# Steps of the norms' transpositions, the MLP's first weights, and the loads of attention's first position terms, placed anew in a four-layer vision kernel

## The chip, the cores and the metric

One core of a Trainium2 chip runs the whole program. The metric is the device time of one execution in microseconds (us), as the median of several runs. A core has five engines that run side by side, each with its own queue of instructions: TensorE (PE in the profile; PEld is its loading of weights), VectorE (DVE), ScalarE (ACT), GpSimd (POOL) and SyncE (SP), which here issues nearly all DMAs. Work moves between HBM and the on-chip SBUF by DMA. Products are accumulated in PSUM[...].

## The reference

The input is one image of 48 x 48 tokens (T = 2304) with C = 768 channels. Four layers follow each other, all in f32. The change touches the first, and three loads of the third.

```python
# layer 0: a transformer block, 12 heads of 64
xn  = layernorm(x, ln1_g, ln1_b)
q, k, v = split(xn @ qkv_w + qkv_b)
attn = (q * scale) @ k.T + rel_h[..., :, None] + rel_w[..., None, :]
out = softmax(attn) @ v
x   = x + out @ proj_w + proj_b
xn2 = layernorm(x, ln2_g, ln2_b)
x   = x + gelu(xn2 @ mlp_w1 + mlp_b1) @ mlp_w2 + mlp_b2     # 768 -> 3072 -> 768
# layer 1: rfft2, a block-diagonal complex MLP over 8 blocks of 96, softshrink, irfft2, + x
# layer 2: projections of x, then 12 steps of a 3x3 depthwise convolution with gates, and an output product
# layer 3: as layer 1
```

`rel_h` and `rel_w` are products of q with windows of two small tables of relative positions.

## The kernel before

**Blocks and products.** Tokens go in six blocks of TB = 384; two of them make a superblock, sb = 0, 1, 2. Each large product is taken as a 2 x 2 block product with seven multiplications instead of eight, so operands need sums of blocks first (`block_sums`, `combine`: four additions each), and results are put together on DVE from PSUM. `rows_in_seven` (L167) is this for the v product and for the output projection: seven products n = 0 to 6, three row tiles t each, so 21 calls a superblock. A call is three 128x384 products, which the profile counts as six PE instructions, into one of six PSUM tiles, an eviction by DVE or ACT, and then `between()`. After n = 1, 4, 5 and 6 `emit` adds on POOL and stores.

**Norms.** A layer norm of one block is made of `layernorm_rows` for three row tiles of 128 tokens (two statistics L74, small operations L76 to L89, one subtraction and multiplication L90, nearly all on DVE) and of `transpose_norm` (L94): for each of six channel groups, three transpositions on PE (`n_tp`) into one PSUM tile, and an eviction by ACT or DVE in turn that applies gain and bias. `prepare` does both for one block.

**qkv (`qkv_phase`, L258).** For each superblock the v product is followed by `q_and_k`: six pairs of heads `pr`, seven products n each. In sb = 0 the pair's weights are loaded and combined on POOL in place (L359 to L366), and are kept in HBM for the later superblocks. The position terms' products (`rel_h` L488, `rel_w` L480) are steps in a list that `advance()` takes one by one, after products n = 2 and 5 of pairs from pr = 2 on, and between the calls of the v product. `rel_h` fills the tile `rh` (one buffer, L491) and stores it. `prepare(sb + 1, 0)` stands after pair 3 and `prepare(sb + 1, 1)` after pair 5 (L411 to L417). x comes in six tiles of one buffer each, from a pool inside this phase (L290).

**Into attention.** `load_ahead` (L1457) loads the first keys and values at pair 4 of the last superblock. Past the last pair it opens a pool `at_a` for two query tiles `qt` and three tiles of position terms `bt` and loads them (L1464 to L1469). A bound on the scores, from the maxima of q and k, gives `flag` (L557 to L561), after which the last steps of position terms are issued (L562). Every engine reads `flag` and branches (L1487, L1488) to `attention_bounded` or `attention_any`; the given data take the first. Attention works on products of keys and queries (L657), position terms by a one-hot matrix (L667), exponentials on ACT (L669), and products with values (L688).

**Projection and MLP.** `proj_phase` (L835) makes 63 calls of `rows_in_seven` and stores x with the residual in `xr_d`. `mlp_phase` (L920) opens its pools, and calls `prepare(0, 0)`, `prepare(0, 1)`, which load rows of `xr_d`. `first_layer` (L970) loads the weights of step f (L980) and multiplies (L996).

**What sets the order.** The program gives instructions in source order. The framework's scheduler then orders each engine's queue by source order and by when it expects operands and buffers to be free, so that an instruction can come out ahead of its line's place; `tc.keep_in_program_order` pins one. Tiles of one tag share the given number of buffers, and memory of a closed pool is given to pools opened later. It is the scheduler too that puts in the waits.

## Time and profile before

| | us |
|---|---|
| median of 3 runs (lowest, highest) | 3575.01 (3571.93, 3576.77) |
| the profiled execution | 3578.66 |
| its span, first to last instruction | 3576.8 |

| stage, us from the span's start | length | PE busy |
|---|---|---|
| qkv phase and entry, 0 to 461 | 461 | 446.4 |
| attention, 461 to 1470 | 1009 | 1006.8 |
| projection, 1470 to 1597 | 127 | 122.8 |
| entry to the MLP, 1597 to 1622 | 25 | 18.1 |
| MLP, 1622 to 2595 | 973 | 973.0 |
| layer 1, 2595 to 2845 | 250 | 245.6 |
| layers 2 and 3, 2845 to 3577 | 732 | 701.0 |

In the timeline's lines below, the first two columns are start and length in us; then come the engine, the line of the kernel, the operation, the tiles written and read, the shape, and the count. In brackets stands the time that the engine sat idle before, and what ended it. PE busy counts instructions in flight: at a low granted clock an instruction takes longer, and PE still counts as busy. Times of the profile are of one execution.

### The profile page before, as it was taken

To read this page: it belongs to the slowest core of one execution; us is meant where nothing else is said; L and a number is where in the kernel's file an instruction comes from. 1 tells how busy PE (TensorE), PEld (TensorE's weight loads), DVE (VectorE), ACT (ScalarE), POOL (GpSimd) and SP (SyncE) were. 2 spreads that over 40 slices of the span, in tenths; PEclk is the share of its full clock that TensorE was granted. 3 is DMA by queue.
4 is the path that set the end of the run, shared out by engine and by line. 5 is a ranking of instruction groups with operands and counts; after the bars stand their busy time and mean duration, and the time that the engine had idled before them with its cause. 6 is when DMAs were issued, how large, how long until landed. Compare 5 with 4: busy or idle time off the path is not lost.

```text
span 3576.8 us, 52953 instructions
## 1 busy us (share of the span) xinstructions
PE 3513.7 (98%) x21274; PEld 2148.0 (60%) x21274; DVE 2004.7 (56%) x3015; ACT 1141.4 (32%) x1735; POOL 680.8 (19%) x572
## 2 busy tenths in 40 slices
PE   9999999999999999989999999999999998999998
PEld 5666554444444444555555555555578767996685
DVE  7644466766676776654234324232345578996554
ACT  1321254555555555203101210121023265223332
POOL 3211102111111110250000000000023303981121
PEclk9999999999999999999999999999999999999999
DMA  7555556655545443344346334533554403104456
GB/s 276 201 187 189 187 156 173 187 145 152 164 123 148 125 125 87 111 150 139 106 131 184 114 110 126 164 112 112 156 134 119 109 21 105 34 27 100 107 143 132
DMA packets 281171, 480.38 MB, mean 134 GB/s; under 512 B 37250, under 2 KB 234466, under 8 KB 274708
## 3 DMA queue, kind: packets, MB, share of 16 engines
q1 hardware_dynamic: 265322, 455.95, 43.8%
q10 hardware_dynamic: 15594, 20.94, 2.0%
q8 instruction: 171, 2.80, 0.3%
q14 instruction: 84, 0.69, 0.1%
HBM read 330.82 MB, written 145.98 MB: 133 GB/s over the span
## 4 chain that ended last, share of the span: by engine, by line
PE 91%; DVE 3%; POOL 2%; DMA 2%; ACT 1%; issue 1%; SPq 0%; ACTq 0%; DVEq 0%; POOLq 0%
PE p L996 14%; PE p L1059 13%; PE s L657 12%; PE av L688 12%; PE qk L375 6%; PE c L1223 4%; PE s L667 3%; PE c L1323 3%; PE v L180 3%; PE pj L180 3%; PE f_u L1682 2%; PE f_z L1666 2%; PE f_z L1667 2%; PE so L1410 2%; PE f_x L1631 2%; POOL t L1331 1%
## 5 line engine op out<-in xcount | busy, mean ns | idle before, releaser
L677 DVE TENSOR_TENSOR acc<-acc,p 128x928 f32<-128x928 f32 (+1 forms) x480 | 560.2, 1167 | 263.6 <-ACT p L669 222.6
L669 ACT ACTIVATE p<-s 128x928 f32<-128x928 f32 (+1 forms) x540 | 506.5, 940 | 491.6 <-PE s L667 470.0
L657 PE MATMUL s<-qt,kv 64*128 64x464 f32 (+1 forms) x2160 | 521.9, 559 | 7.5 <-DMA qt<-q_d 5.5
L1059 PE MATMUL p<-w,h 128*128 128x384 f32 x1512 | 492.3, 486 | 0.0
L688 PE MATMUL av<-p,kv 128*64 128x464 f32 (+1 forms) x2160 | 442.9, 554 | 0.0
L1059 PEld LDWEIGHTS p<-w,h 128*128 128x128 f32 x1512 | 285.6, 190 | 199.0 <-issue 4.2
L667 PE MATMUL s<-bt,oneh 64*128 64x464 f32 (+1 forms) x1080 | 400.8, 731 | 0.7 <-DMA bt<-rh_d 0.7
L688 PEld LDWEIGHTS av<-p,kv 128*64 128x64 f32 x2160 | 147.0, 137 | 261.9 <-issue 249.6
L657 PEld LDWEIGHTS s<-qt,kv 64*128 64x128 f32 x2160 | 203.0, 187 | 164.7 <-issue 153.4
L996 PE MATMUL p<-x2nT,w 128*128 128x384 f32 x864 | 294.0, 491 | 4.0 <-POOL rr L1035 4.0
L1323 PE MATMUL c<-H,bands 128*48 128x96 f32 x5632 | 245.1, 247 | 10.2 <-DVE th L1261 8.3
L375 PE MATMUL qk<-xnT,wqk 128*128 128x384 f32 x756 | 249.8, 487 | 0.3 <-DMA wqk<-wqk_d 0.3
L1323 PEld LDWEIGHTS c<-H,bands 128*48 128x48 f32 x5632 | 235.2, 124 | 20.3 <-issue 8.7
L996 PEld LDWEIGHTS p<-x2nT,w 128*128 128x128 f32 x864 | 165.2, 192 | 121.3 <-POOL rr L1035 4.2
L996 PE MATMUL p<-xT,w 128*128 128x384 f32 x648 | 220.8, 486 | 0.0
L1035 POOL TENSOR_TENSOR rr<-rr,ml_b 128x1152 f32<-128x1152 f32 x12 | 31.8, 2653 | 946.1 <-DMA rr<-xr_d 855.1
L991 ACT ACTIVATE h<-h,ml_b 128x384 f32<-128x384 f32 x144 | 88.5, 616 | 346.7 <-DVE h L1011 173.5
L375 PEld LDWEIGHTS qk<-xnT,wqk 128*128 128x128 f32 x756 | 141.4, 190 | 93.4 <-issue 0.9
L1331 POOL TENSOR_TENSOR t<-s,c 128x768 f32<-128x768 f32 x80 | 144.4, 1829 | 179.4 <-DVE s L1294 166.5
L996 PEld LDWEIGHTS p<-xT,w 128*128 128x128 f32 x648 | 123.1, 190 | 85.9
L667 PEld LDWEIGHTS s<-bt,oneh 64*128 64x128 f32 x1080 | 106.9, 188 | 105.7 <-issue 102.9
L1666 PE MATMUL f_z<-f_w,f_o 97*96 97x96 f32 x800 | 134.1, 249 | 0.0
(336 smaller groups left out, 4601.2 us busy)
## 6 DMA issues: line engine op xcount, KB each, us to landing
w<-w1s_d SPq DMA_DIRECT2D x36, 768.0 KB
w<-w2s_d SPq DMA_DIRECT2D x36, 768.0 KB
w<-w1s_d SPq DMA_DIRECT2D x36, 576.0 KB
w<-in_mlp_w_dram SPq DMA_DIRECT2D x27, 768.0 KB
yu<-f_ys SPq DMA_DIRECT2D x48, 384.0 KB
wqk<-wqk_d SPq DMA_DIRECT2D x12, 1344.0 KB
bt<-rw_d SPq DMA_DIRECT2D x72, 174.0 KB
bt<-rh_d SPq DMA_DIRECT2D x72, 174.0 KB
```

Source lines behind the costliest of these rows:

```text
L180: nc.tensor.matmul(p[:, :TB], lhsT=rhs[n][:, c, t * P : (t + 1) * P], rhs=w[:, c, :], start=c == 0, stop=c == NC2 - 1)
L375: nc.tensor.matmul(p[:, :TB], lhsT=w[:, n, c, :], rhs=ops[sb][n][:, c, :], start=c == 0, stop=c == NC2 - 1)
L657: nc.tensor.matmul(ps[:, s, :n], lhsT=keys[pr % 2][rows, kt * P : (kt + 1) * P], rhs=held(c)[rows, :n], start=True, stop=False)
L667: nc.tensor.matmul(ps[:, s, :n], lhsT=oneh[rows, b % 2, :], rhs=bts[b // 2][rows, j, :n], start=False, stop=True)
L669: nc.scalar.activation(p, ps[:, :, :n], AF.Exp)
L677: nc.vector.tensor_tensor(probs[c], probs[c], p, ALU.add)
L688: nc.tensor.matmul(avs[c][rows, : size(c)], lhsT=vals[pr % 2][:, kt, rows], rhs=p[:, s, :], start=kt == 0, stop=kt == NT - 1)
L996: nc.tensor.matmul(p[:, :TB], lhsT=w[n][:, c, :], rhs=rhs[n][:, c, :], start=c == 0, stop=c == NC2 - 1)
L1059: nc.tensor.matmul(ps[t][:, :TB], lhsT=hs[left, f][:, t * P : (t + 1) * P], rhs=wt[:, f % KW2, :], start=f == 0, stop=f == NF2 - 1)
L1323: nc.tensor.matmul(ps[r0 : r0 + G, k // 4, cols], lhsT=bands[:, n - GC, i, :] if gr else bands0[:, n, i, :], rhs=H[:, n, :, d : d + NPR], ...
L1331: GP.tensor_tensor(t, sc[:, ch], c1[:, m0 : m0 + GC].unsqueeze(2).to_broadcast([P, GC, RR, NPR]), ALU.mult)
L1666: nc.tensor.matmul(out, lhsT=o1[:, j, 1:3, :].rearrange("c r h -> c (r h)"), rhs=w2t[:, b, 0, :], start=True, stop=False)
```

## The change

It does seven things.

1. `transpose_norm` becomes a generator that stops after each channel group. In the qkv phase from sb = 1 on its transpositions are pinned on PE. `q_and_k` makes the norm at pairs 1 and 3, and takes its steps after products: of pairs 2 and 4 (n = 1, 3, 4, 6), and of 3 and 5 (n = 0, 1).
2. The norm of the first MLP superblock moves into the projection, with the statistics (L74) and the transpositions pinned: `mlp_norms` holds what `mlp_phase` had, and `proj_phase` takes a step of it at the calls named in `norm_at`. The first two weights of the MLP are loaded at calls 40 and 41.
3. The tiles of x become pairs in a pool `at_x` of three buffers, which lives through attention; `bt` takes the same buffers. `qt` lies in the pool of attention's constants.
4. In the last superblock `rh` has three buffers, in the place of `rw`.
5. The last steps of position terms come ahead of the bound.
6. In sb = 0, block sums that n = 4 and later need are issued at n = 2 of the v product, the windows of the position tables are loaded after it, and the weights of pairs 0 and 1 are made in its `emit`, with POOL's additions pinned for pairs 0 to 2.
7. Three loads of biases in the scan phase (layer 2) are pinned on SP.

```diff
-def layernorm_rows(nc, pool, xt, name):
+def layernorm_rows(nc, pool, xt, name, pin=lambda ins: ins):
...
-        nc.vector.bn_stats(out=st[:, i, :], in_=xt[:, i * half : (i + 1) * half])
+        pin(nc.vector.bn_stats(out=st[:, i, :], in_=xt[:, i * half : (i + 1) * half]))
...
-def transpose_norm(nc, psum, xhs, xnT, ident, g, b, name):
+def transpose_norm(nc, psum, xhs, xnT, ident, g, b, name, pin=lambda ins: ins):
...
-            nc.tensor.transpose(ps[:, t * P : (t + 1) * P], xhs[t][:, cc * P : (cc + 1) * P], ident)
+            pin(nc.tensor.transpose(ps[:, t * P : (t + 1) * P], xhs[t][:, cc * P : (cc + 1) * P], ident))
...
+        yield
...
         wv = qkv_w.rearrange("(c p) n -> p c n", p=P)
-        Xs, ops = {}, {}
+        Xs, ops, pairs = {}, {}, [None]
...
                 i = (2 * sb + half) * 3 + t
-                Xs[i] = xp.tile([P, C], F32, tag="x", name=f"x_{i}", bufs=6)
+                if i % 2 == 0:
+                    pairs[0] = xb.tile([P, 2, C], F32, tag="xb", name=f"x_{i}")
+                Xs[i] = pairs[0][:, i % 2]
                 if i == 1:
...
-            transpose_norm(nc, lambda name: pool.tile([P, 512], F32, tag=tag, name=name), xhs, ops[sb][:, :, half, :], ident, g, b, f"n1_{blk}")
+            return transpose_norm(nc, lambda name: pool.tile([P, 512], F32, tag=tag, name=name), xhs, ops[sb][:, :, half, :], ident, g, b, f"n1_{blk}", tc.keep_in_program_order if sb else lambda ins: ins)
...
                 nc.sync.dma_start(v_d[:, 3 * blk : 3 * blk + 3, cols], o)
+                if sb == 0 and len(made) < 2:
+                    make_qk(len(made))
...
+        made = []
+        def make_qk(pr):
+            w = w_tile(f"wqk_0_{pr}").rearrange("p (n c f) -> p n c f", n=7, c=NC2)
+            wb = wp.tile([P, NC2, P], F32, tag="wb", name=f"wb_{pr}", bufs=2)
+            lo, hi = slice(pr * P, (pr + 1) * P), slice(C + pr * P, C + (pr + 1) * P)
+            nc.sync.dma_start(w[:, 0:2].rearrange("p a c f -> p (a c) f"), wv[:, :, lo])
+            nc.sync.dma_start(w[:, 6], wv[:, NC2:, hi])
+            nc.sync.dma_start(wb, wv[:, :NC2, hi])
+            pin = tc.keep_in_program_order if pr < 3 else lambda ins: ins
+            combine(nc.gpsimd, (w[:, 0], w[:, 1], wb, w[:, 6]), w[:, 3], w[:, 2], w[:, 5], w[:, 4], pin)
+            made.append(w)
...
-            made = []
...
-                    w = w_tile(f"wqk_{sb}_{pr}").rearrange("p (n c f) -> p n c f", n=7, c=NC2)
-                    wb = wp.tile([P, NC2, P], F32, tag="wb", name=f"wb_{pr}", bufs=2)
-                    lo, hi = slice(pr * P, (pr + 1) * P), slice(C + pr * P, C + (pr + 1) * P)
-                    nc.sync.dma_start(w[:, 0:2].rearrange("p a c f -> p (a c) f"), wv[:, :, lo])
-                    nc.sync.dma_start(w[:, 6], wv[:, NC2:, hi])
-                    nc.sync.dma_start(wb, wv[:, :NC2, hi])
-                    combine(nc.gpsimd, (w[:, 0], w[:, 1], wb, w[:, 6]), w[:, 3], w[:, 2], w[:, 5], w[:, 4])
-                    made.append(w)
+                    if pr > 1:
+                        make_qk(pr)
+                    w = made[pr]
...
                         step()
+                    elif sb + 1 < NSB and (pr in (2, 4) and n or pr in (3, 5) and n < 2):
+                        next(norm, None)
                 for o, d, m in ((q[:, pr], q_d, qms), (kt, k_d, kms)):
...
                     ahead(0)
-                if pr == NC2 and sb + 1 < NSB:
-                    prepare(sb + 1, 0)
-                    load_x(sb + 1, 1)
+                if pr in (1, 3) and sb + 1 < NSB:
+                    norm = prepare(sb + 1, pr // 2)
             if sb == 0:
                 nc.sync.dma_start(wqk_d[NC - 1], made[NC - 1])
-            if sb + 1 < NSB:
-                prepare(sb + 1, 1)
...
-            prepare(0, 1, first_sums)
+            finish(prepare(0, 1, first_sums))
...
-            tc.keep_in_program_order(V.tensor_tensor(w[:, 4], w[:, 1], w[:, 2], ALU.subtract))
-            tc.keep_in_program_order(V.tensor_tensor(w[:, 5], w[:, 0], a21, ALU.subtract))
-            V.tensor_tensor(x12, x22, x12, ALU.subtract)
-            V.tensor_tensor(t4, x21, t2, ALU.subtract)
...
-            windows = load_windows(nc, atc, relT)
-            tc.keep_in_program_order(V.tensor_scalar(kb, qkb[:, NC : 2 * NC], HD**-0.5, None, ALU.mult))
-            rm = qp.tile([P, 2], F32, tag="rm", name="rm")
-            tc.keep_in_program_order(V.tensor_reduce(rm, windows.rearrange("p t k s -> p t (k s)"), axis=AX.X, op=ALU.max, apply_absolute_value=True))
+            V.tensor_scalar(kb, qkb[:, NC : 2 * NC], HD**-0.5, None, ALU.mult)
...
-            v_rows(0, lambda n: w[:, n])
+            def weights(n):
+                if n == 2:
+                    V.tensor_tensor(w[:, 4], w[:, 1], w[:, 2], ALU.subtract)
+                    tc.keep_in_program_order(V.tensor_tensor(w[:, 5], w[:, 0], a21, ALU.subtract))
+                    V.tensor_tensor(x12, x22, x12, ALU.subtract)
+                    V.tensor_tensor(t4, x21, t2, ALU.subtract)
+                return w[:, n]
+            v_rows(0, weights)
+            windows = load_windows(nc, atc, kp, relT)
+            rm = qp.tile([P, 2], F32, tag="rm", name="rm")
+            V.tensor_reduce(rm, windows.rearrange("p t k s -> p t (k s)"), axis=AX.X, op=ALU.max, apply_absolute_value=True)
...
-        with tc.tile_pool(name="qkv_o", bufs=1, side="right") as op:
+        with tc.tile_pool(name="qkv_o", bufs=1, side="right") as op, ExitStack() as after:
...
+            rw_stack, pools = ExitStack(), []
+            rwp = rw_stack.enter_context(tc.tile_pool(name="qkv_r", bufs=1, side="right"))
...
                     if (n, hh) == (0, 0):
-                        tiles["rh"] = op.tile([P, KP, 2, 2, TB], F32R, tag="rh", name=f"rh_{sb}_{cp}")
+                        if sb + 1 < NSB:
+                            tiles["rh"] = op.tile([P, KP, 2, 2, TB], F32R, tag="rh", name=f"rh_{sb}_{cp}")
+                        else:
+                            if cp == 0:
+                                rw_stack.close()
+                                pools.append(after.enter_context(tc.tile_pool(name="qkv_h", bufs=3, side="right")))
+                            tiles["rh"] = pools[0].tile([P, KP, 2, 2, TB], F32R, tag="rh", name=f"rh_{sb}_{cp}")
                     by_row, at = tiles.pop(("h", cp, n, hh)), tiles["rh"]
...
+            while steps or ready:
+                advance()
...
-            while steps or ready:
-                advance()
...
+        norm_at = {28, *range(39, 45), 47, *range(56, 63)}
...
-            rows_in_seven(nc, pm, f"pj_{sb}", rhs, lambda n: w[:, n - 2] if n > 1 else pw[:, n], xp, emit)
+            calls = itertools.count(21 * sb)
+            def between():
+                n = next(calls)
+                if n in norm_at:
+                    next(norm, None)
+                if n in (40, 41):
+                    first_weights(0, n - 40)
+            rows_in_seven(nc, pm, f"pj_{sb}", rhs, lambda n: w[:, n - 2] if n > 1 else pw[:, n], xp, emit, between)
+        finish(norm)
...
-def mlp_phase(tc, ident, w1s_d, b1, w2, w2s_d, b2, ln_g, ln_b, xr_d, xa_d, follow_in):
+def mlp_norms(tc, stack, ident, ln_g, ln_b, xr_d, w1s_d):
+    nc = tc.nc
+    cp = stack.enter_context(tc.tile_pool(name="ml_c", bufs=1, side="left"))
+    pt = stack.enter_context(tc.tile_pool(name="ml_t", bufs=2, space=PSUM))
+    wp = stack.enter_context(tc.tile_pool(name="ml_w", bufs=4, side="left"))
+    g = load_cols(nc, cp, ln_g, NC, "ln2_g")
+    b = load_cols(nc, cp, ln_b, NC, "ln2_b")
+    ops, ws = {}, {}
+    def first_weights(sb, f):
+        ws[sb, f] = []
+        for i, n in enumerate(S1W):
+            wt = wp.tile([P, 4, NC2, P], F32, tag="w", name=f"w1_{sb}_{f}_{i}")
+            nc.sync.dma_start(wt[:, :n], w1s_d[f, :, 3 * i : 3 * i + n])
+            ws[sb, f] += [wt[:, k] for k in range(n)]
+    def prepare(xp, sb, half):
+        blk = 2 * sb + half
+        if half == 0:
+            ops[sb] = [cp.tile([P, NC, 2, TB], F32, tag="x2nT", name=f"x2nT_{sb}")]
+            ops[sb] += [cp.tile([P, NC2, TB], F32, tag=f"x{n}", name=f"x{n}_{sb}") for n in ("T1", "T2", "T4")]
+        xhs = []
+        for t in range(3):
+            xt = xp.tile([P, C], F32, tag="x", name=f"ml_x_{blk}_{t}", bufs=6 if sb else 4)
+            r0 = (3 * blk + t) * P
+            nc.sync.dma_start(xt, xr_d[r0 : r0 + P, :])
+            xhs.append(layernorm_rows(nc, xp, xt, f"ln2_{blk}_{t}", lambda ins: ins if sb else tc.keep_in_program_order(ins)))
+        X, t1, t2, t4 = ops[sb]
+        yield
+        yield from transpose_norm(nc, lambda name: pt.tile([P, 512], F32, tag="t", name=name), xhs, X[:, :, half, :], ident, g, b, f"n2_{blk}", lambda ins: ins if sb else tc.keep_in_program_order(ins))
+        if half:
+            ops[sb] = block_sums(nc, X, t1, t2, t4)
+    return cp, wp, pt, ops, (first_weights, ws), prepare
+def mlp_phase(tc, opened, b1, w2, w2s_d, b2, xr_d, xa_d, follow_in):
...
-                w = []
-                for i, n in enumerate(S1W):
-                    wt = wp.tile([P, 4, NC2, P], F32, tag="w", name=f"w1_{sb}_{f}_{i}")
-                    nc.sync.dma_start(wt[:, :n], w1s_d[f, :, 3 * i : 3 * i + n])
-                    w += [wt[:, k] for k in range(n)]
+                if (sb, f) not in ws:
+                    first_weights(sb, f)
+                w = ws.pop((sb, f))
...
-                bias = load_bcast(nc, wp, b0_d, NA + NCR, "bias")
-                bias1 = load_bcast(nc, tp, b1_d, NA + NCR, "u")
+                bias = load_bcast(nc, wp, b0_d, NA + NCR, "bias", pin=tc.keep_in_program_order)
+                bias1 = load_bcast(nc, tp, b1_d, NA + NCR, "u", pin=tc.keep_in_program_order)
...
-                cb = load_bcast(nc, wp, cb_d, NN, "cb")
+                cb = load_bcast(nc, wp, cb_d, NN, "cb", pin=tc.keep_in_program_order)
...
+    xb = at_stack.enter_context(tc.tile_pool(name="at_x", bufs=3, side="left"))
...
+    qbs = [atc.tile([P, QB], F32, tag=f"qt{i}", name=f"qt{i}") for i in range(2)]
...
-        pool = at_stack.enter_context(tc.tile_pool(name="at_a", bufs=1, side="left"))
-        qbs = [pool.tile([P, QB], F32, tag=f"qt{i}", name=f"qt{i}") for i in range(2)]
-        bts = [pool.tile([P, KJ, QB], F32R, tag=f"bt{g}", name=f"bt{g}") for g in range(NG3)]
+        bts = [xb.tile([P, 2 * C], F32R, tag="xb", name=f"bt{g}")[:, : KJ * QB].rearrange("p (j n) -> p j n", j=KJ) for g in range(NG3)]
...
-    proj_phase(tc, x, pw, ps_d, a["proj_b"], oT, xr_d)
+    mlp_stack = ExitStack()
+    mlp = mlp_norms(tc, mlp_stack, ident, a["ln2_g"], a["ln2_b"], xr_d, w1s_d)
+    with tc.tile_pool(name="pj_n", bufs=3, side="right") as xp:
+        proj_phase(tc, x, pw, ps_d, a["proj_b"], oT, xr_d, itertools.chain(*(mlp[-1](xp, 0, half) for half in range(2))), mlp[-2][0])
...
-    mlp_phase(tc, ident, w1s_d, a["mlp_b1"], a["mlp_w2"], w2s_d, a["mlp_b2"], a["ln2_g"], a["ln2_b"], xr_d, xa_d, follow_in)
+    mlp_phase(tc, mlp, a["mlp_b1"], a["mlp_w2"], w2s_d, a["mlp_b2"], xr_d, xa_d, follow_in)
+    mlp_stack.close()
```

`finish(steps)` runs a generator to its end. The qkv phase's first block and the later MLP norms use it.

## The prediction

> **What bounds the kernel now.** I read the page's busy times first, then the PE waits, then stage windows over the four places that the diff touches, then PE's and SP's order of time inside these.
>
> ```profile
> PE 3513.7 (98%) x21274; PEld 2148.0 (60%) x21274; DVE 2004.7 (56%) x3015; ACT 1141.4 (32%) x1735; POOL 680.8 (19%) x572
> ```
>
> PE is the bound: 3576.8 - 3513.7 = 63 us is all that it idles. The diff changes no product and no size, so it can only win PE's idle time and PE time spent at a low clock, or add to them. The windows (length; then busy us and count of PE, PEld, DVE, ACT, POOL; granted clock; DMA share; GB/s) show where both are:
>
> ```profile
> 201.92:223.14 21.22, 19.40 (x79) 11.68 (x78) 9.47 (x15) 6.79 (x11) 3.61 (x3) 1.00 0.96 337
> 436.44:460.96 24.52, 16.43 (x89) 13.26 (x87) 10.33 (x18) 10.89 (x14) 1.93 (x4) 0.79 0.80 213
> ...
> 1471.00:1597.50 126.50, 122.97 (x379) 71.46 (x379) 70.73 (x136) 6.80 (x16) 63.04 (x23) 1.00 0.49 156
> 1597.50:1609.88 12.38, 5.51 (x37) 3.70 (x36) 9.07 (x9) 4.03 (x6) 7.86 (x3) 0.97 0.77 239
> 1609.88:1620.73 10.85, 10.85 (x25) 6.13 (x26) 4.82 (x6) 3.66 (x4) 0.00 (x0) 0.72 0.53 197
> ```
>
> See the clock of 0.79 and 0.72: the second and the last look busy, but the same products take longer there. PE's order of time, into attention and into the MLP:
>
> ```profile
> 439.79 0.20 PE L558 MATMUL bound<-pz,onec 128*1 128x12 f32 x2 [1.83 <-DVE pz L552]
> 439.92 1.60 PE L496 MATMUL rh<-qh,windows 128*96 128x96 f32 x16
> 447.05 1.92 PE L657 MATMUL s<-qt,kv 64*128 64x464 f32 x4 [5.53 <-DMA qt<-q_d]
> 448.38 0.93 PE L667 MATMUL s<-bt,oneh 64*128 64x464 f32 x1
> 450.04 0.72 PE L667 MATMUL s<-bt,oneh 64*128 64x464 f32 x1 [0.72 <-DMA bt<-rh_d]
> ...
> 1536.52 6.22 PE L180 MATMUL pj<-pj_wt,oT 128*128 128x384 f32 x18 [1.39 <-DVE pj_u L185]
> ...
> 1597.50 0.82 PE L99 MATMUL n_tp<-ident,ml_x 128*128 128x128 f32 x6
> 1598.75 0.89 PE L99 MATMUL n_tp<-ident,ml_x 128*128 128x128 f32 x6 [0.43 <-ACT x2nT L103]
> ...
> 1609.88 7.13 PE L996 MATMUL p<-x2nT,w 128*128 128x384 f32 x12 [4.04 <-POOL rr L1035]
> ```
>
> and SP's issues that PE waits for there:
>
> ```profile
> 443.69 0.33 SPq L609 DMA_DIRECT2D qt<-q_d  x1
> 444.07 0.42 SPq L580 DMA_DIRECT2D bt<-rw_d  x1
> ...
> 1605.37 2.06 SPq L980 DMA_DIRECT2D w<-w1s_d  x4
> ```
>
> Attention's first loads go out at 443.69, when k's last store has landed (the chain of waits has DMA k_d<-kT, 437.88 for 5.74, then these issues): their tiles lie in memory that the qkv pools free. The MLP's first weights go out at 1605.37. The 4.04 us are put down to POOL L1035, which ends at 1609.29; no product reads rr, so I take the real wait to be these weights.
>
> **What the Trainium skill says.** "TensorE: Matmul & The Clock Gate", Part 1: about 3.4 us without work halve PE's clock, and about 3.4 us of work restore it. The trace agrees in kind: after idles of 5.53 and 4.04 us the clock is 0.79 and 0.72; after gaps of 1.4 us in the projection it is 1.00. The same page ("Architectural detail") has DVE and ACT strictly first in, first out, and PE's products too: a pinned operation that waits holds all behind it. Here DVE sat 7.54 us before L74 until ml_x landed at 1527.95. "SBUF — State Buffer", "Who interferes with whom": a DVE operation with two SBUF inputs and a reading GpSimd operation block each other for their whole length. Here L154 takes 3.78 us beside POOL's rr and 1.36 alone, and L86, 128x1, took 2.55 beside L862.
>
> **The change part by part**, against the span of 3576.8 us. One instruction of a 128x384 product costs 0.3225 us (36 in 11.61 at the start of the projection); three of a transposition's 128x128 products about 0.33 us when packed between others (six in 0.65 at 115.85).
>
> (a) First v products. PE waits 0.53 (28.13, DVE L449) and 1.31 us (35.52, DVE L189). Between 25.87 and 35.38 DVE does the windows' two copies (0.93, 0.95), the row maximum (0.53) and four sums of 1.34 before it takes up v's evictions. The change moves windows and maximum behind the v products and the four sums behind n = 1. The four sums then stand at n = 2, 5.4 us of DVE with six PSUM tiles of 1.935 us as cover. Gain 1.8. The windows are first read at 91.73, and rel's two loads now wait for an output tile, near 64: cover 25 us; without it they would hold SP's queue, where sb 1's x and pair 2's weights (issued 51.68 to 61.31 now) stand. make_qk's combinations, pinned on POOL, are 4 x 1.00 us after each v emit; the first weight is wanted at 58.84 and should be done near 38. Bounds 0 to 2.5.
>
> (b) Norm 1 of sb 1 and 2. sb 1's 36 transpositions already lie between products (115.85, 147.87) and lose nothing; the pins keep that. sb 2's run as a block from 215.47 to 223.30: 7.8 us, and 36 x 0.109 = 3.9 of it is work. Gain 3.9. They become PE's pinned steps one or three products apart (1.94 us), and an eviction takes 0.67. PE stands still if the norm is late, but its statistics stood on DVE at 38 to 48 for sb 1 while the first step comes near 90. The x pairs share three buffers, the same 18 KB; x_8 now waits for x_3 too, free at 24.5. Bounds 3 to 3.9.
>
> (c) Into attention. From 436.44 to 460.96 PE does 32 rh instructions (16 in 1.52: 3.0), the bound, and nine tiles of scores (0.99 each in steady state: 8.9); 24.5 - 11.9 = 12.6 us are lost. Afterwards bt lies in x's buffers, free since sb 1, and qt in its own, so all 13 loads can land before 440; kv's first load stands after pair 4 in the source (five pairs of 14 us after 348.96: near 419) and went out at 372.09, so SP takes such loads early. The rh tiles no longer share one buffer with a store in between (ACT waits 5.60 us at 443.45). What is late next is the flag: rh ends near 440.2 (POOL's copies, 1 us a step), bound and DVE's two operations 0.5, PE's load of the flag 0.86 (440.4 in the trace), branch 0.09: PE starts near 442. The exponential's table load (1.28) and three PSUM tiles cost about 0.5: nine tiles end at 451.4 instead of 460.96, gain 9.5. Worst: the flag now comes behind all rh and a gap of 3 us or more cools the clock (3 us, as at 1609.88 below), and bt lands at 445: gain 4. I take 8. Attention's load of q into oT stands behind the rh stores on SP; its products are wanted 20 us after the entry (nine tiles of scores, 4.8 of values, six tiles more).
>
> (d) Projection and MLP entry. From 1471.00 to 1620.73 PE does 378 + 24 product instructions (129.7) and 36 transpositions (3.9): 133.6 of 149.7, 16.1 lost. It is 3.5 in three DVE waits (1536 to 1551, where DVE is busy 27.91 of 28.05 us with six rows of norm), 8.4 of idle around the transpositions and for the weights, 3.1 of slow clock (24 instructions in 10.85 instead of 7.74), and 1 spread over the projection. In the changed kernel the first of the two norms is pinned at call 28, which ends 29 x 1.935 after 1471.0: 1527.1, when ml_x lands now (1527.95; its store's way is unchanged). The other is pinned at 47. Each is three row tiles of some 2.8 us on DVE (two L74 of 0.55, L90 of 0.67, eight small ones of 0.1 to 0.2): 8.4, beside one or two evictions of 0.56 a call. Six PSUM tiles cover 11.6 us. Transpositions go to calls 39 to 44 and 56 to 61. The weights of two MLP steps (2 x (768 + 576) KB) are issued at calls 40 and 41, on SP ahead of the second norm's loads: 2.7 MB at some 200 GB/s are 13 us, and calls 41 to 47 last as long. If they take longer, DVE waits at call 47. Block sums follow call 62: t1 is ready earlier, t3 and t2 cost 1.35 + 1.35, or 3.8 + 1.35 beside POOL's last addition; PE has two products (3.9 us) until it wants t2: up to 1.5 lost. ACT's first copy may wait for the last store (near +6.7), again under six tiles. I take 3 us left: gain 13. Bounds 6 (DVE falls 4 us behind at both norms) to 15.5.
>
> (e) The scan's three pinned loads: 1.3 us of SP issue move from 2623.9 (one waited until 2643.8) to about 2822; bias is first used at 2838.26. Gain 0, bounds -2 to +1.
>
> Sum: 1.8 + 3.9 + 8 + 13 = 26.7, taken as 26.5. Span 3576.8 - 26.5 = 3550.3. The profiled execution took 3578.66, 3.65 over the median of 3575.01; the same gain below that median is 3548.5. Ends of the terms: 30.7 gives 3544.3; 1 + 3 + 4 + 10 = 18 gives 3557. About 0.2% (7.1 us) is what a measurement of this kernel can tell from no change.
>
> **The rivals.** *Given back in the projection* (0.17): the pinned norms and transpositions put DVE behind there, and (d) brings 3 instead of 13: 3558.5, from 3555 to 3569. For it: 27.91 of 28.05, and blocks of 3.3 to 3.8 us beside POOL. Against: half as many rows at a time. *Entry still late* (0.13): bt or flag come as now, or the change's own tiles don't free the loads, (c) brings 2: 3552 to 3557, with 3554.5. For it: SP's queue is in order and the loads' line stands after the rh stores. Against: kv's load at 372.09. *Slower* (0.08): at calls 28 and 47 DVE waits for ml_x in front of PSUM's evictions. Price: beyond 11.6 us, one us of PE for each. A wait of W at each costs 2 x (W + 8.4 - 11.6); it decides against the change from W = 20 us on (33.6 lost, the gain and 7.1 more), and at 25 us gives 3548.5 + 43.6 = 3592. For it: the pins forbid DVE to go round them, and 2.7 MB of weights come just before. Against: the trace has 9.9 us from POOL's addition (1518.09) to the statistics (1527.95), most of them over before call 28.
>
> **How the numbers follow.** The forecast has 0.62, its own range 3544 to 3557. The range 3543 to 3563 takes in the late entry and most of the first rival; outside are that rival's end and the slower case, with a little of the forecast. Faster: 0.62 + 0.13 + 0.13 of the first rival = 0.88; within 0.2%: its 0.04; slower 0.08.
>
> **What would show it.** Right: no block of L99 after the projection; w1's loads near 1555; PE's first scores between 441 and 444 at a clock of 1.00; first MLP product within 1 us of the last of the projection; none of the DVE waits above. Wrong: PE waits for pinned transpositions on DVE L90, waits in the projection over 3 us, a gap of more than 4 us at the branch, or new idle after 1620, where I expect a shift alone.

## The result, and the profile after

The changed kernel took 3559.27 us (median of 6 runs, 3556.20 to 3560.74) beside 3574.76 us for the kernel before (6 runs, 3571.93 to 3576.77): a ratio of 0.9953, 95% interval 0.9943 to 0.9963. It is 15.5 us faster. Forecast were 26.5 us; 3559.27 lies inside the range of 3543 to 3563, but outside the likeliest case's own 3544 to 3557.

The profiled execution of the changed kernel took 3558.49 us, its span is 3556.6. PE's line of busy times:

```profile
PE 3505.5 (99%) x21274; PEld 2145.6 (60%) x21274; DVE 2007.9 (56%) x3015; ACT 1136.2 (32%) x1733; POOL 683.4 (19%) x572
```

PE's 21274 instructions are the same number; they take 8.2 us less, in part because more of them run at full clock (the mean granted clock is 0.995 where it was 0.993), and PE idles for 51.1 us instead of 63.1. The windows of the changed kernel, at the entry into attention, the projection, the entry into the MLP and the entry into layer 1 (columns as before: length; busy us and count of PE, PEld, DVE, ACT, POOL; granted clock; DMA share; GB/s):

```profile
433.34:450.18 16.84, 12.86 (x90) 8.14 (x88) 9.10 (x17) 10.71 (x14) 1.94 (x4) 1.00 0.75 232
1459.47:1585.57 126.10, 126.10 (x414) 75.18 (x414) 80.87 (x142) 10.73 (x22) 62.52 (x23) 1.00 0.55 179
1585.57:1597.50 11.93, 11.03 (x34) 6.58 (x35) 7.91 (x8) 2.83 (x4) 9.89 (x3) 1.00 0.75 241
2588.08:2605.00 16.92, 12.54 (x53) 8.15 (x54) 4.30 (x10) 2.58 (x6) 2.15 (x3) 0.80 0.96 220
```

The entry into attention has shrunk from 24.52 to 16.84 us, in this execution at a clock of 1.00. The projection is busy for all of its 126.10 us, with 36 transpositions inside it, and nothing of the clock of 0.72 is left at the MLP's entry. The last window is the surprise: a clock of 0.80 at a place that the change does not touch. PE's order of time in the changed kernel:

```profile
435.36 1.86 PE L523 MATMUL rh<-qh,windows 128*96 128x96 f32 x16 [0.50 <-POOL qh L533]
437.15 0.20 PE L588 MATMUL bound<-pz,onec 128*1 128x12 f32 x2
440.27 1.01 PE L685 MATMUL s<-qt,kv 64*128 64x464 f32 x3 [2.92 <-DMA k_d<-kT]
...
1536.94 0.49 PE L104 MATMUL n_tp<-ident,ml_x 128*128 128x128 f32 x3
1537.27 2.10 PE L186 MATMUL pj<-pj_wt,pj_xT 128*128 128x384 f32 x6
...
1586.47 4.14 PE L1048 MATMUL p<-x2nT,w 128*128 128x384 f32 x12 [0.90 <-DVE pj_o L195]
...
2588.82 2.15 PE L139 MATMUL f_first<-f_w,f_fh 96*96 96x384 f32 x6 [0.74 <-DVE rr L1091]
2593.67 1.92 PE L1685 MATMUL f_x<-f_fh,f_yt 96*96 96x96 f32 x10 [2.70 <-DMA f_yt<-yu]
2595.37 2.77 PE L139 MATMUL f_first<-f_w,f_fh 96*96 96x384 f32 x4
```

Attention's first scores come behind a wait of 2.92 us. The bracket names the store of k, but PE reads the flag just before, and that read can start only when DVE has written it. These are lines of another view (count; least, median and greatest length in ns; first and last start in us):

```profile
L591 DVE TENSOR_SCALAR flag<-mx x1: 141/141/141, 438.6 to 438.6; 1x1 int32<-1x1 f32 x1
L1537 PEldq TENSOR_LOAD <-flag x1: 892/892/892, 438.8 to 438.8; - x1
```

The flag is written at 438.72, PE has read it at 439.65 and branched at 440.00, and the scores start at 440.27: most of the wait is for the flag. Three transpositions stand between products at 0.33 us from start to start (1536.94 to 1537.27), and the first MLP product follows 0.90 us behind the projection. In layer 1 PE waits 2.70 us for a load of `f_yt`, and the four products after it take 2.77 us. The kernel before has neither; here are PE and then SP's issues of the same place in it:

```profile
2617.22 1.01 PE L1631 MATMUL f_x<-f_fh,f_yt 96*96 96x96 f32 x10
2618.07 1.46 PE L133 MATMUL f_first<-f_w,f_fh 96*96 96x384 f32 x4
```

```profile
2610.43 0.87 SPq L1588 DMA_DIRECT2D f_yt<-yu  x2
2615.12 0.38 SPq L1044 DMA_DIRECT2D xa_d<-rr  x1
```

and SP's issues in the changed kernel:

```profile
2569.53 10.48 SPq L1608 DMA_DIRECT2D yu<-f_ys  x4
2588.11 0.33 SPq L1642 DMA_DIRECT2D f_yt<-yu  x1
2588.70 0.39 SPq L1096 DMA_DIRECT2D xa_d<-rr  x1
```

Before, two loads go out at 2610.43, 4 us ahead of the end of PE's last MLP product (2614.49). After, the first goes out at 2588.11, 0.03 us behind that end (2588.08).

Two profiles of the kernel before and three of the changed one, taken in all, give the stages below. A stage runs from the first PE product of one group to that of the next (us).

| stage | before | after | mean gain | forecast |
|---|---|---|---|---|
| start to first v product | 13.0, 15.2 | 14.3, 13.0, 12.9 | 0.7 | none |
| to first qk product | 45.9, 45.4 | 43.9, 43.9, 43.9 | 1.7 | (a) 1.8 |
| to last qk product | 377.3, 377.3 | 374.8, 374.7, 374.4 | 2.6 | (b) 3.9 |
| to first projection product | 1034.9, 1031.2 | 1026.5, 1026.5, 1025.4 | 6.9 | (c) 8 |
| to `f_first`, layer 1 | 1144.2, 1142.2 | 1129.4, 1129.4, 1129.4 | 13.9 | (d) 13 |
| to first `f_o` | 4.5, 4.5 | 9.1, 9.3, 8.7 | -4.6 | 0 |
| to the end | 957.1, 955.7 | 958.7, 959.6, 954.3 | -1.1 | (e) 0 |
| span | 3576.8, 3571.5 | 3556.6, 3556.4, 3548.9 | 20.2 | 26.5 |

### The profile page after: what moved, and what is told of

The parts are those of the page before. It is cut to its first block, busy times and chain, and to the rows that moved or that the text cites. A ratio compares the mean times of both kernels' runs of the same rounds, so it can differ in the third digit from the quotient of the medians.

```text
span 3556.6 us, 52951 instructions
## 1 busy us (share of the span) xinstructions
PE 3505.5 (99%) x21274; PEld 2145.6 (60%) x21274; DVE 2007.9 (56%) x3015; ACT 1136.2 (32%) x1733; POOL 683.4 (19%) x572
## 4 chain that ended last, share of the span: by engine, by line
PE 90%; DVE 3%; DMA 3%; ACT 2%; POOL 1%; issue 1%; SPq 0%; ACTq 0%; DVEq 0%; POOLq 0%
PE p L1111 14%; PE p L1048 14%; PE s L685 12%; PE av L716 11%; PE qk L391 6%; PE c L1273 4%; PE pj L186 3%; PE c L1373 3%; PE s L695 3%; PE v L186 3%; PE f_u L1736 2%; PE so L1460 2%; PE f_z L1721 2%; PE f_z L1720 2%; PE f_x L1685 2%; PE f_o L1699 1%
## 5 line engine op out<-in xcount | busy, mean ns | idle before, releaser
L1373 PE MATMUL c<-H,bands 128*48 128x96 f32 x5632 | 244.6, 247 | 10.2 <-DVE th L1311 8.3
```

The source lines that it names most:

```text
L1373: nc.tensor.matmul(ps[r0 : r0 + G, k // 4, cols], lhsT=bands[:, n - GC, i, :] if gr else bands0[:, n, i, :], rhs=H[:, n, :, d : d + NPR], ...
```

## The experiments

Theory: the forecast's four gains are there, and 5 us are given back at layer 1's entry because of where the MLP's pools now lie. In the changed kernel the weight pool `ml_w` opens ahead of `ml_x`. From the tiles' sizes, `f1_y` (three buffers of 7.5 KB behind 19 KB of `f1_c`) reaches over the end of `ml_c` into `ml_w`, whose last tile the last MLP product reads; before, it reached into `ml_x`. Rivals: the wait is chance, or comes from another part, or another wait would take its place.

### The load buffers in pools of their own

```diff
-    cp, yp = (... (("c", 1), ("y", bufs)))
+    parts = bufs if name == "f1" else 1
+    cp, *yps = (... (("c", 1), *((f"y{i}", bufs // parts) for i in range(parts))))
...
-            yts[group, kc] = yp.tile(...)
+            yts[group, kc] = yps[len(yts) % parts].tile(...)
```

> The changed kernel, with the three buffers for layer 1's first loads (f_yt) taken from three pools of one buffer instead of one pool of three; nothing else differs, the places in memory are the same. Theory (the pool of three overlaps the MLP's weight pool, so its first load waits for the MLP's last product): the first f_yt load is issued when yu's last stores have landed, some 4 us before PE's last MLP product ends; the wait of 2.70 us of PE L1685 and the slow clock after it are gone; 3559.3 - 5.3 = 3554. Rival (the load is late for another reason, or another wait takes its place): a wait of 2 to 3 us stays at layer 1's entry, 3559. Second rival (the 5.3 us are won at the entry but given back inside layer 1): first output group 5 us earlier, 3558 to 3559.

3552.42 us (5 runs, 3550.90 to 3554.31), ratio to before 0.9939 (0.9925 to 0.9952). SP's issues and PE's order of time:

```profile
2567.67 10.08 SPq L1608 DMA_DIRECT2D yu<-f_ys  x4
2581.74 0.87 SPq L1643 DMA_DIRECT2D f_yt<-yu  x2
```

```profile
2586.57 2.15 PE L139 MATMUL f_first<-f_w,f_fh 96*96 96x384 f32 x6 [0.74 <-DVE rr L1091]
2588.55 1.01 PE L1686 MATMUL f_x<-f_fh,f_yt 96*96 96x96 f32 x10
2589.40 1.46 PE L139 MATMUL f_first<-f_w,f_fh 96*96 96x384 f32 x4
```

The first two loads go out together again, 4.1 us ahead of the last MLP product's end (2585.82), the wait is gone and the four products take 1.46 us. From `f_first` to the first `f_o` it is 4.4 us instead of 9. By the tiles' sizes the places in memory are the same, so it is the pool as a whole that waited: only its third buffer reaches into `ml_w`, but the first load taken from it carried the wait. The theory holds; the time fell by more than 5 us, so a second set was run beside the changed kernel.

> The changed kernel with layer 1's three load buffers in three pools, the same kernel as y_own_pools, beside the changed kernel on the same chip. Theory (the entry of layer 1 is worth 5.3 us, the rest of the 7 us seen first is chance: a wait for f_gt in layer 3 that takes 2.3 or 4.7 us, and the scan's first products at full or half clock): 5 us below the changed kernel, 3553 to 3555. Rival (all 7 us come of the pools): 3552.

> The changed kernel, unaltered, timed beside the other three. Theory: 3558 to 3560, the f_yt wait of 2.7 to 3 us at layer 1's entry; the scan's first ten products take 3.2 or 4.9 us after the same wait of 2.01, by chance. Rival (the slow clock there belongs to this kernel): 4.9 for the third time.

3553.23 us (3549.25 to 3554.01; ratio 0.9935, 0.9921 to 0.9948) beside 3554.98 for the changed kernel (3550.71 to 3559.26; ratio 0.9945, 0.9932 to 0.9959). In this set the medians are 1.8 us apart, where 5 were expected, and the intervals overlap; the changed kernel itself came out below the 3558 to 3560 expected of it. Over all runs it is 3552.8 (10 runs) against 3558.6 (12 runs). What repeats is the stage: 4.4 us in both profiles with own pools, 9.1, 9.3 and 8.7 in the three of the changed kernel, with waits of 2.70, 2.91 and 2.87 us. The stage is worth 4.6 us; the exact share in the median stays uncertain within 2 to 6 us.

> The changed kernel once more, unaltered, for a second profile. Theory (the entries into attention, MLP and layer 1 are set by the program's order): first values, first MLP product and first outputs of layer 1 within 0.5 us of the first profile's distances, the 2.70 us wait for f_yt at layer 1's entry there again. Rival (that wait is chance): it is gone or below 1 us, and the span some 4 us shorter.

3558.17 us, span 3556.4, wait 2.91: the wait is not chance. The first MLP product and layer 1's first outputs come where they were expected, but attention's first values do not: they stand 19.24 us behind the last qk product where the first profile has 17.16. PE's first scores, and the window that in the first profile took 16.84 us at a clock of 1.00:

```profile
438.78 1.92 PE L685 MATMUL s<-qt,kv 64*128 64x464 f32 x4 [2.80 <-DMA k_d<-kT]
```

```profile
431.97:450.88 18.91, 15.58 (x89) 9.98 (x87) 9.98 (x17) 11.05 (x14) 1.94 (x4) 0.82 0.78 252
```

Behind much the same wait, 2.80 us, the clock fell here. In the third profile of the changed kernel it fell too, for a shorter time: 18.10 us to the first values. So this entry is not set by the program's order alone.

### The two pool lines swapped in the kernel before

```diff
-        tc.tile_pool(name="ml_x", bufs=3, side="left") as xp,
         tc.tile_pool(name="ml_w", bufs=4, side="left") as wp,
+        tc.tile_pool(name="ml_x", bufs=3, side="left") as xp,
```

> The kernel before with the MLP's pools of weights and of rows opened in the other order, two lines swapped, nothing else. Theory (the place of the weight pool decides both: its memory is free during the projection, and layer 1's load buffers then overlap it): the MLP's first weights are issued during the projection and the 4.04 us wait and the slow clock behind it shrink, 5 to 7 us gained; the first f_yt load waits for the last MLP product, 5 us lost with a wait of 2 to 3 us on f_yt: 3571 to 3575 in sum. Rival (the wait of 4.04 is for POOL's rr or the norm, not for weights): nothing gained at the MLP's entry, 3579 to 3580.

3601.03 us (5 runs, 3594.56 to 3603.73), ratio 1.0070 (1.0056 to 1.0084): the expected sum was off by 26 us or more. PE's order of time:

```profile
1605.94 0.66 PE L99 MATMUL n_tp<-ident,ml_x 128*128 128x128 f32 x2 [17.08 <-DVE ln_q L86]
...
1625.49 1.01 PE L996 MATMUL p<-xT,w 128*128 128x384 f32 x1 [4.30 <-DVE xT L155]
...
2630.59 1.09 PE L1631 MATMUL f_x<-f_fh,f_yt 96*96 96x96 f32 x10 [3.05 <-DMA f_yt<-yu]
```

and SP's issues:

```profile
1489.50 2.96 SPq L980 DMA_DIRECT2D w<-w1s_d  x4
...
1596.63 25.64 SPq L961 DMA_DIRECT2D ml_x<-xr_d  x12
...
2624.68 0.34 SPq L1588 DMA_DIRECT2D f_yt<-yu  x1
```

Both parts of the theory are there: the weights go out at 1489.50 instead of 1605.37, and the `f_yt` wait of 3.05 us appears in the kernel before, from two swapped lines. What was not foreseen is a third effect: the norm's rows go out only at 1596.63, where the kernel before had the first of them landed by 1527.95, and PE stands 17.08 us for the norm. Whichever pool takes the place that is free during the projection loads early; the other is late. The change has both early because it gives the first norms a pool of their own (`pj_n`) on the other side.

### The projection and the MLP's entry undone

```diff
-    mlp = mlp_norms(tc, mlp_stack, ident, ...)
-    with tc.tile_pool(name="pj_n", bufs=3, side="right") as xp:
-        proj_phase(tc, x, pw, ps_d, ..., mlp[-2][0])
+    proj_phase(tc, x, pw, ps_d, a["proj_b"], oT, xr_d)
...
+        prepare(0, 0)
+        prepare(0, 1)
```

The two `prepare` lines are in `mlp_phase`, which opens its pools in the old order.

> The changed kernel with the projection and the MLP's entry as they were before (norms as a block behind the projection, weights issued there, the MLP's pools in their old order). Theory (the change wins 15 us there and its new pool order costs 5.3 at layer 1's entry): 3559.3 + 15 - 5.3 = 3569, and no wait for f_yt at layer 1's entry. Rival (the loss at layer 1's entry comes from elsewhere in the change, or is chance of one execution): the wait of 2.7 us stays, 3559.3 + 15 = 3574.

3563.82 us (6 runs, 3561.78 to 3565.33), ratio 0.9967 (0.9955 to 0.9979): faster than either expectation. There is no `f_yt` wait; two loads go out at 2595.01, and `f_first` to `f_o` is 4.5 us, so the loss at layer 1 does belong to (d). From the first projection product to `f_first` it takes 1143.7 us, 14.3 more than the changed kernel. Net 9.7 us should remain by stages; the times show 5.2 (against 3558.6 over all runs). Part of the difference sits in stages that the undoing does not touch (1025.3 us through attention where the changed kernel has 1026.1 in the mean, 0.5 at the start), and it is not resolved further.

This kernel also tells what PE waits for at the MLP's entry. PE, POOL and SP:

```profile
1594.54 7.07 PE L1024 MATMUL p<-x2nT,w 128*128 128x384 f32 x12 [4.31 <-issue]
```

```profile
1591.33 3.77 POOL L1063 TENSOR_TENSOR rr<-rr,ml_b 128x1152 f32<-128x1152 f32 x1 [2.55 <-DMA rr<-xr_d]
```

```profile
1590.02 2.11 SPq L1008 DMA_DIRECT2D w<-w1s_d  x4
```

The first product starts while POOL is still at rr, so it does not wait for that. It starts 4.5 us after the weights' first issue, as it did in the kernel before (1605.37 and 1609.88).

### The first weights' calls taken out

```diff
-                if n in (40, 41):
-                    first_weights(0, n - 40)
```

> The changed kernel without the two calls that issue the first two weight sets of the MLP at calls 40 and 41 of the projection; they are asked for at the MLP's own place in the program, from the same pool. Theory (the pool is open and its memory free, so the loads go out during the projection anyway): 3559, first MLP product within 1 us of the projection's last. Rival (the calls bring the loads forward): the loads go out after the norm's loads, near 1575, PE waits 3 to 5 us and loses 3 more to a slow clock, 3565 to 3567.

3556.23 us (4 runs, 3553.39 to 3559.01), ratio 0.9955 (0.9938 to 0.9971): no loss. First this kernel's issues of the weights, then those of the changed kernel:

```profile
1477.33 3.57 SPq L972 DMA_DIRECT2D w<-w1s_d  x4
```

```profile
1465.27 0.34 SPq L974 DMA_DIRECT2D w<-w1s_d  x1
...
1479.78 2.38 SPq L974 DMA_DIRECT2D w<-w1s_d  x3
```

Call 40 ends near 1539 in the changed kernel (two transpositions' steps: 1536.94 and 1539.21). The loads run ahead of it in both kernels, since their memory is free from the projection's start. It is the pool, not the calls, that brings them forward.

### The qkv transpositions as blocks again

```diff
-                    elif sb + 1 < NSB and (pr in (2, 4) and n or pr in (3, 5) and n < 2):
-                        next(norm, None)
...
-                if pr in (1, 3) and sb + 1 < NSB:
-                    norm = prepare(sb + 1, pr // 2)
+                if pr == NC2 and sb + 1 < NSB:
+                    finish(prepare(sb + 1, 0))
...
+            if sb + 1 < NSB:
+                finish(prepare(sb + 1, 1))
```

> The changed kernel with the transpositions of norm 1 of the second and third sub-block as unpinned blocks, as they were before. Theory (a block of 36 transpositions leaves PE idle for half its length): 2.5 to 4 us slower, 3562 to 3563, with 7.8 us of transpositions in a row near 215. Rival (the scheduler places them between products all the same, since x now comes earlier): 3559, no such block.

3561.32 us (5 runs, 3558.22 to 3561.86), ratio 0.9962 (0.9948 to 0.9975). First to last qk product takes 377.1 us, as before, against 374.6. A part of the block:

```profile
216.74 1.09 PE L104 MATMUL n_tp<-ident,x 128*128 128x128 f32 x6 [0.22 <-DVE xnT L106]
218.06 1.08 PE L104 MATMUL n_tp<-ident,x 128*128 128x128 f32 x6 [0.23 <-DVE xnT L106]
```

Six transpositions take 1.32 us from start to start, against 2 x 0.33 = 0.66 between products. The theory holds at its lower end: 2.5 us by the stage, 2.8 by the medians. This run takes away the pins on the transpositions (in lines not shown) together with their places between products; which of the two counts is not separated.

### The parts of the entry into attention

Two kernels undo one half each. The first puts `x`, `qt` and `bt` back in pools as before:

```diff
-                if i % 2 == 0:
-                    pairs[0] = xb.tile([P, 2, C], F32, tag="xb", name=f"x_{i}")
-                Xs[i] = pairs[0][:, i % 2]
+                Xs[i] = xp.tile([P, C], F32, tag="x", name=f"x_{i}", bufs=6)
...
-        bts = [xb.tile([P, 2 * C], F32R, tag="xb", name=f"bt{g}") ... for g in range(NG3)]
+        pool = at_stack.enter_context(tc.tile_pool(name="at_a", bufs=1, side="left"))
+        qbs = [pool.tile(...) for i in range(2)]
+        bts = [pool.tile(...) for g in range(NG3)]
```

> The changed kernel with the six x tiles back in qkv's own pool and attention's first q and bias tiles (qt, bt) back in a pool that opens behind it, as before; the three rh buffers and the order of bound and flag stay. Theory (the entry is won by loads that no longer wait for qkv's memory): first scores some 5 us later with a wait on a load of qt or bt and a slow clock behind it, 3559.3 + 7 = 3566. Rival (the rh buffers or the flag's order carry the entry): 3559 to 3561.

The second leaves the last rh tiles one buffer:

```diff
-    tc.tile_pool(name="qkv_h", bufs=3, side="right")
+    tc.tile_pool(name="qkv_h", bufs=1, side="right")
```

> The changed kernel with one buffer instead of three in the own pool of the last rh tiles. Theory (the stores of rh come between the tiles again, ACT waits for them, and the flag stands behind the last tile on DVE): 1 to 3 us slower, 3560 to 3562. Rival (these buffers carry the entry's gain of 8 to 9 us): 3565 or more. Second rival (nothing hangs on them): 3559, first scores where they are.

With the late loads: 3564.75 us (9 runs, 3561.98 to 3566.80), ratio 0.9975 (0.9965 to 0.9985), 6.2 over the changed kernel's 3558.6 of all runs. Its PE:

```profile
442.85 1.92 PE L683 MATMUL s<-qt,kv 64*128 64x464 f32 x4 [6.66 <-DMA qt<-q_d]
446.31 0.72 PE L693 MATMUL s<-bt,oneh 64*128 64x464 f32 x1 [0.86 <-DMA bt<-rh_d]
```

`qt` goes out at 439.81 and PE waits for it; the first scores come 11.0 us behind the last qk product instead of 7.2. The loads' memory carries the entry. With one rh buffer: 3559.89 us (5 runs, 3558.47 to 3560.89), ratio 0.9961 (0.9947 to 0.9975). ACT, then PE:

```profile
439.56 1.61 ACT L206 CAST rh<-rh 96x384 fp32r<-96x384 f32 x4 [5.71 <-DMA rh_d<-rh]
```

```profile
442.27 1.92 PE L685 MATMUL s<-qt,kv 64*128 64x464 f32 x4 [5.81 <-DVE rh L208]
```

ACT waits 5.71 us for a store of rh, DVE's subtractions stand behind it, and the scores come 10.2 us behind the last qk product. In the profile this costs 3.2 us up to the projection; the medians show 1.3, below what they can tell. So both halves are needed: with either alone the first scores are nearly as late as before (10.9 and 10.8 us).

> The kernel before once more, unaltered, for a second profile. Theory (its first profiled execution was 4 us above its median by chance, spread over stages that the change does not touch): span 3571 to 3575, the entries into attention (24.5 us from the last qk product to the first values) and into the MLP (12.4 + 10.9 us) within 1 us of the first profile, and the scan's first products at full clock. Rival (the first profile's entries were long by chance, so that the gains read there are too large): the entries are 3 to 4 us shorter in sum.

3573.25 us, span 3571.5. From the last qk product to the first values it is 23.7 us (24.9 by the same count in the first profile), from the last projection product to the MLP's first 12.3 (12.7): 1.5 in sum, between the two expectations. Most of the first profile's excess is in attention itself (first scores to first projection product 1024.0 against 1020.4).

### The flag asked for first, in the kernel with own pools

```diff
-            while steps or ready:
-                advance()
             ps = pm.tile([P, 512], F32, tag="m", name="bound")
             ...
             V.tensor_scalar(flag, mx, SAFE, None, ALU.is_lt)
+            while steps or ready:
+                advance()
```

> y_own_pools with bound and flag asked for before the last steps of the rh terms, as before, instead of behind them. Theory (in the changed kernel DVE takes the flag's two operations up behind three subtractions of rh, 1.1 us late, and PE's first scores wait for the flag): flag some 1 us earlier, first scores 1 us earlier, 0.5 to 1 us below y_own_again. Rival (PE now waits for pz in front of the rh products, as the kernel before did for 1.83 us, and what is won on DVE is lost on PE): equal to y_own_again or up to 1 us slower.

3549.03 us (5 runs, 3547.59 to 3550.90), ratio to before 0.9923 (0.9909 to 0.9936): the fastest of all. PE's order of time:

```profile
435.09 0.20 PE L586 MATMUL bound<-pz,onec 128*1 128x12 f32 x2 [2.16 <-DVE pz L580]
435.22 1.98 PE L523 MATMUL rh<-qh,windows 128*96 128x96 f32 x16
438.55 1.92 PE L685 MATMUL s<-qt,kv 64*128 64x464 f32 x4 [1.35 <-DVE rh L208]
```

The profile sides with the rival: PE waits 2.16 us for `pz` in front of the rh products, DVE has the flag at 435.86, but the scores wait for DVE's last reading of rh (438.30) and come 7.5 us behind the last qk product, no earlier than the 7.2 of the changed kernel. Its span, 3547.7, is that of y_own_again (3547.4). Why its median is 4.2 us lower is not shown by these profiles; the intervals of the two ratios overlap.

## Why the prediction was right, and where it was not

**Direction and range: right, the range in part by luck.** Each of the four gains stands at its place, most of it for the reason given; (b) and (c) were sized too high, and a loss was missing. The number alone would mislead: 3559.27 is nearly what the rival *given back in the projection* named (3558.5). But the projection gives nothing back, as its window shows. The loss stands at layer 1, which no rival named, and the upper part of the range was there for other cases.

**(a) Right.** 1.7 us measured for 1.8, and neither the 0.53 nor the 1.31 us wait is left. No run undoes this part alone.

**(b) Mechanism right, size off: 2.6 for 3.9.** The block did go. From the second superblock's first qk product to the third's, the time shrinks from 147.03 to 143.66 us, 3.4; 0.3 of what is missing there is a wait for a load of `wqk` (216.27). But in all three profiles of the changed kernel a new wait of some 0.75 us came up (at 162.51 in the first), where the rw products wait for an eviction of v; it is gone in without_b. A block's length less its work overstates what is won: the steps cost something elsewhere.

**(c) Mechanism right, a little oversized: 6.9 for 8, bounds 4 to 9.5.** No late load is left; late_bt and one_rh show the two mechanisms that the forecast named. Of the 6.9 us, 3.7 lie before the first scores, 2.4 between them and the first values, and 0.8 in the rest of attention, where the two profiles of the kernel before differ by 2.6. The window itself gave 7.7 in the first pair of profiles, and 6.1 in the mean of all. Two things were mis-sized. The flag was what is late next, as forecast, but it took longer: from the end of the bound's products (437.35) to the flag (438.72) it was 1.4 us, not 0.5, because DVE took three subtractions of rh first. And the clock of 1.00 at the first scores, named as a sign of being right, was there in one of three profiles of the changed kernel; the forecast had the slow clock only in its worst case. To ask for the flag first gained nothing (y_flag_first), since rh's evictions are then as late.

**(d) Right: 13.9 for 13, by a partly wrong path.** No DVE waits, no cold clock, 0.90 us to the MLP's first product. But the weights went out at 1465 and 1480, not near 1555 at calls 40 and 41: the forecast took a call in the source for the moment of issue, though it had used the opposite in (c) (keys and values that go out ahead of their line). That the 4.04 us of before, put down to POOL's rr, were the weights' is borne out by without_d. In before_swapped, where the weights go out early, the first product (1611.57) follows the transpositions without a wait, and the 4.30 us a little later are for a sum of blocks (`xT`).

**(e) Right in value only.** The scan's loads stayed at 2617.84 to 2623.06 and did not move to 2822.

**What failed: "new idle after 1620, where I expect a shift alone".** The forecast followed SBUF forwards, to see whose memory the new pools take, and not to the next tenants of the places that moved. The swap of `ml_w` and `ml_x` was in the diff, and `f1_y` over it in the source. It costs 4.6 us to the first `f_o`, shown by taking it away (y_own_pools), by its absence in without_d, and by making it in the kernel before (before_swapped).

**The balance.** The four terms' 26.7, less 4.6 at layer 1, 1.3 in (b), 1.1 in (c), 0.1 in (a) and 1.1 in the rest, plus 0.9 in (d) and 0.7 at the start, are the 20.2 us between the mean spans of the profiled executions, to 0.1. The medians of the first set show 15.5, those of the last 22.2 (3577.17 against 3554.98). The runs do not take that remainder apart further; single executions of one kernel spread by several us, and the last section shows pieces of that.

## What to carry to other kernels

When pools move, follow each place to its next tenant, past the code that the diff touches: what matters is which engine reads the old tile last, and that the first tile of a pool may wait for all that the whole pool overlaps. Where buffers are needed one after another and only the last reaches into busy memory, a pool for each cost nothing here and took the wait away. Ask of every early load what frees its memory; the line where it is issued said little here.

## What the runs showed of the hardware

The scan's first products follow the same wait of 2.01 us in all 14 profiles, and take 3.23 us in seven of them and 4.80 or 4.92 in the other seven. The second profile of the kernel before, and y_own_again:

```profile
2821.16 3.23 PE L1223 MATMUL c<-wsc,xh 128*112 128x357 f32 x10 [2.01 <-DVE c L1176]
```

```profile
2795.02 4.92 PE L1273 MATMUL c<-wsc,xh 128*112 128x357 f32 x10 [2.01 <-DVE c L1226]
```

The granted clock is 1.00 in the one kind and 0.51 at first in the other (changed kernel, 2804.20 to 2806.70). The changed kernel itself has both: 4.92, 4.92 and 3.23. A gap of 2 us here costs either nothing or 1.6 to 1.7 us more, and single executions of one kernel differ by it.

Attention's entry does the same behind a longer wait. In eight profiles PE waits 2.80 to 2.92 us for the first scores. In four of them (the changed kernel's first, y_own_again, without_d, late_w1) the clock stays at 1.00, and the first values come 17.1 to 17.2 us behind the last qk product. In the other four (after_again, after_timed, y_own_pools, without_b) it falls to 0.50, and they come after 17.9 to 19.2 us. The `f_yt` wait of 2.70 to 3.17 us was followed by the slow clock in all eight profiles that have it. So in these runs the length of a gap between 2 and 3 us did not decide alone whether the clock falls.

The Trainium skill, "TensorE: Matmul & The Clock Gate", Part 1, says that the clock follows a window of activity that runs freely and doesn't start with the kernel, so that the moment of a change varies with where in it the first product falls. That outcomes differ behind equal gaps agrees in kind; but the page's figure of some 3.4 us for one idle window is longer than all of these gaps, and here 2.01 us were enough in half of the executions.

Another piece of the spread between executions is the wait for `f_gt` in layer 3, 4.8 and 2.2 us in the two profiles of the kernel before. What decides between its values is open.
